# A four-layer graph network on one core: the ends of its first two layers, rearranged

## The chip, the cores and the metric

The kernel runs on one core of one Trainium2 chip, in a single launch. The metric is device time in microseconds (us). The runs of the kernel before took 5248.02, 5226.67 and 5222.31 us, with 5226.67 as their median. Durations below come from one further execution, taken with the hardware profiler.

The engines are called as in the profile: PE multiplies matrices (PEld is its loading of weights), DVE and ACT work on vectors, POOL issues the indirect DMAs that gather rows by index, and SP issues the direct DMAs. Each engine runs its own queue of instructions in order, and waits on semaphores for the others.

## What is computed

There are 6250 nodes with 256 features each, and 100000 edges (`src`, `dst`), sorted by `dst`. Four graph layers follow one another, and every one is added to its input and normalised:

```python
x = layernorm(x + L0(x))   # h = relu(layernorm(x)*gamma + beta); agg = mean of h[src] over the edges of each dst
                           # L0 = agg @ W_l.T + b_l + h @ W_r.T
x = layernorm(x + L1(x))   # attention over the edges, 8 heads, softmax over the edges of each src:
                           # s = q[src] . k[dst]; p = exp(s - max); out[src] = sum p/denom * v[dst]; out @ Wo + bo
x = layernorm(x + L2(x))   # two GAT layers of 4 heads over the edges and self loops, grouped by dst, gelu
x = layernorm(x + L3(x))   # mean over the edges of dst, two products, residual, relu
```

Layer 0 groups its edges by `dst`, in which order the input has them. Layer 1 groups them by `src`, so the kernel has to order the edges anew before layer 1 may begin.

## The kernel before

**Blocks and pieces.** Nodes are worked in 50 blocks of 125 (`NB`, `B`). The edges that end in a block have up to 16 columns of 128 slots (`CM`); what doesn't fit goes to two further columns that ten blocks share (`SH`, `GB`). A column is fetched with one indirect DMA that gathers 128 rows (`gather`, L873). A piece is a few columns of one block: 6, 6 and 4 in layer 0 (150 pieces), four times 4 in layer 1 (200 pieces). For a piece, `one_hots` (L882, DVE) makes matrices that say which slot belongs to which node of the block, and PE multiplies them with the gathered rows, which sums the rows by node in a PSUM tile `ps`. A piece is a generator; `run_pass` (L1476) starts one per step and advances every one that is under way, twice in the last ten steps. A scheduler then turns what the generators emit into one queue per engine, by estimated times and by the tiles that come free; a tile name with one buffer is handed to its users in turn.

**Layer 0.** `piece0` gathers rows of `h_table` into one of four tiles `g`. After the last piece of a block comes `finish0`: the mean `agg`; its transposition (`turned`, L856, into PSUM tile `pt`, copied out by ACT in `kept`, L861); the transposition of the block's own `h` (L1527, into `pt`); the product with `w_l` and `w_r` (`product`, L869, 8 matmuls, into PSUM tile `po`); the sum and the layer norm (`norm`, ACT at L839); a transposition of the new `x`; the products for k, v and q (12 matmuls into `po`); and two writes through SP, to `kv_table` and to `q_table` (from tile `qp`, made by `parts_of`, L823 to L826). `pt` and `po` have one buffer each.

**The ordering by source**, `by_source`, is a generator that runs beside layer 0. Its main part goes over 800 columns of 125 edges. For each, DVE makes two one-hot tiles (`oh` L1421, `o1` L1423), ACT scales one of them (`oa` L1425, `ob` L1427, for the last 200 columns `oc` L1437 too), and PE adds their products to a PSUM tile `acc` of two banks (L1432). Each group of four columns yields a cost of 3.6. After the last column DVE decodes `acc` (L1445 to L1469) into `key_s` (the node of each slot), `idx_s` (the row to gather), and the same for the shared columns (`far_s`, `near_s`). The pace is set in `beside(t)`, called after piece t has been started: the ordering is advanced until the costs it has yielded reach a number times t + 1:

```python
            def beside(t):
                if next(work_d, None) is None and t < 2:
                    next(work_d, None)
                while given[0] < 6.9 * (t + 1):
                    with tc.issue_after(last_h.ins) if given[0] < 120 else ExitStack():
                        given[0] += next(work_s, 1e9)
```

**Layer 1.** Every ten blocks `shared1` gathers the shared columns from `kv_table` and `q_table` (tile `gs`), ahead of the first piece of these blocks. `piece1` loads the block's rows of `q_table`, gathers four columns of `kv_table` into one of seven tiles `g`, turns the one-hot matrices on PE (tile `tp`), spreads `q` to the edges with them (PE, tile `qe`, two buffers), multiplies with k (DVE `prod`, L1713), sums and exponentiates (`messages`; the product with v is DVE `msg`, L1668), and sums the messages by node on PE (`ps`). After a block's last piece `finish1` follows: division by the denominators, transposition into `pt`, product with `w_o` into `pt`, sum and norm, and `features` (L1619): a further transposition into `pt`, the product with `w_gat` into `pt`, and the write of the block's row of `hs_tables[0]`, which layer 2 gathers from. `bank()` gives all of these the one buffer of `pt`. The weights `w_o` and `w_gat` are loaded when the pools of layer 1 are opened.

Of the kernel before, what the change touches and what calls it, by code (L numbers as in the profile page):

```python
# [7 lines left out]
F32 = mybir.dt.float32  # L8
I32 = mybir.dt.int32
# [646 lines left out]
def gnn_stack_kernel(ctx: ExitStack, tc: tile.TileContext, ins, out):  # L656
# [59 lines left out]
    for r in range(NR):  # L716
# [4 lines left out]
        c0 = max(0, int(place_of(g0 * GQ * EQ, -1)) // P) if g0 else 0  # L721
        reach.append((c0, min(CM, int(place_of((g1 + 1) * GQ * EQ, 1)) // P + 1)))
    DC = max(c1 for c0, c1 in reach)
    BITS = 12
    FIELD = 1 << BITS
    assert CAP + SH * P < FIELD and NB % 2 == 0
# [6 lines left out]
    with ExitStack() as fast:  # L733
# [21 lines left out]
        idx_s = const.tile([P, NB, CM], I32, name="idx_s")  # L755
        key_s = const.tile([P, NB, CH], F32, name="key_s")

        far_d, near_d, far_s, near_s = (
            const.tile([P, NGR, SH], I32, name=f"{a}_{k}") for k in "ds" for a in ("far", "near")
        )  # L760

        flags = const.tile([P, 8], F32, name="flags")
        nc.vector.memset(flags, 0.0)
        n_first = const.tile([1, 1], F32, name="n_first")
        rdens = const.tile([P, NB, 16], F32, name="rdens")
# [98 lines left out]
        def product(ps, pairs):  # L864
            n = len(pairs) * DK
            i = 0
            for aT, w in pairs:
                for k in range(DK):
                    nc.tensor.matmul(ps, aT[:, k, :], w[:, k, :], start=(i == 0), stop=(i == n - 1))  # L869
                    i += 1  # L870
# [48 lines left out]
        def by_target(pool, psum):  # L919
# [88 lines left out]
            nc.vector.tensor_tensor(ends_sb[:, 0, : EP - 1], ends_sb[:, 0, : EP - 1], ends_sb[:, 1, 1:], op=ALU.is_gt)  # L1008
            nc.vector.tensor_reduce(flags[0:1, 1:2], ends_sb[:, 0, : EP - 1], AX.X, ALU.max)
            nc.vector.tensor_copy(n_first, p_row[:, ND : ND + 1])  # L1010

        last_h = [None]

# [230 lines left out]
        def by_source(pool, work, psum):  # L1244
# [223 lines left out]
            for o, v, n in ((idx_s, low[:, :NM], CM), (far_s, low[:, NM:], SH)):  # L1468
                nc.vector.tensor_scalar(  # L1469
                    o.rearrange("p b c -> p c b"), v.rearrange("p (c b) -> p c b", c=n), float(N - 1), 0.0,  # L1470
                    op0=ALU.min, op1=ALU.max,
                )
            yield 6.0


# [15 lines left out]
        with tc.tile_pool(name="f0", bufs=1) as pool, tc.tile_pool(name="f0w", bufs=2) as work, tc.tile_pool(  # L1491
# [13 lines left out]
                nc.sync.dma_start(out=b_kv[:, k, :], in_=broadcast_rows(ins[f"L1_gnn_b{name}"], D))  # L1505
            sums, shared = {}, [None]

            def bank():
                return psum.tile([P, 512], F32, name="pt")

            def finish0(b):
                ps = sums.pop(b)[:B]
                hp = work.tile([B, 3 * D + 2], BF16, name="hp")
                move(nc.sync, hp, block_rows(h_table, b))
                nc.vector.tensor_scalar(rdeg[:, b, :], ps[:, D:], 1.0, None, op0=ALU.max)
                nc.vector.reciprocal(rdeg[:, b, :], rdeg[:, b, :])
                agg = once.tile([B, D], F32, name="agg")
                nc.scalar.activation(agg, ps[:, :D], AF.Copy, scale=rdeg[:, b, :])
                yield
                pt = turned(bank(), agg)  # L1520
                aT = kept(once, pt, "aT")
                yield
                pt = psum.tile([P, 512], F32, name="pt")[:, : DK * B].rearrange("p (k b) -> p k b", k=DK)
                for k in range(DK):
                    for i in (2, 1, 0):
                        at = i * D + k * P
                        nc.tensor.matmul(  # L1527
                            pt[:, k, :], hp[:, at : at + P], ident_b[:B, :B], start=(i == 2), stop=(i == 0)
                        )
                hT = kept(once, pt, "hT")  # L1530
                yield
                po = psum.tile([B, 3, D], F32, name="po")
                product(po[:, 0, :], [(aT, w_l), (hT, w_r)])
                yield
                o = once.tile([B, D], F32, name="o")
                nc.vector.tensor_add(o, po[:, 0, :], b_l[:B, :])
# [46 lines left out]
            def beside(t):  # L1583
                if next(work_d, None) is None and t < 2:
                    next(work_d, None)
                while given[0] < 6.9 * (t + 1):
                    with tc.issue_after(last_h.ins) if given[0] < 120 else ExitStack():
                        given[0] += next(work_s, 1e9)

            run_pass([(lambda a=a: piece0(*a)) for a in pieces((6, 6, 4))], beside)  # L1590
            for _ in work_s:
# [31 lines left out]
        with tc.tile_pool(name="f1", bufs=1) as pool, tc.tile_pool(name="f1w", bufs=2) as work, tc.tile_pool(  # L1623
            name="f1g", bufs=7
        ) as gp, tc.tile_pool(name="f1p", bufs=1, space=bass.MemoryType.PSUM) as psum:
# [3 lines left out]
            sums, held, shared, late = {}, {}, {}, []  # L1629

            def bank():
                return psum.tile([P, 512], F32, name="pt")

            def finish1(b):
                ps = sums.pop(b).rearrange("p (h c) -> p h c", h=H1)
# [52 lines left out]

            def piece1(b, c0, n):
                if c0 == 0:  # L1690
                    if b % GB == 0:
                        late.append(shared1(b // GB))
                    held[b] = work.tile([B, 3 * D], BF16, name="q")
                    move(nc.sync, held[b], block_rows(q_table, b))
                advance(late)
                q = held[b]
                g = gp.tile([P, 4, 2 * D], F32, name="g")
                for i in range(n):
                    gather(g[:, i, :], kv_table[:, :], idx_s[:, b, c0 + i : c0 + i + 1])
                st = one_hots(work, key_s[:, b, c0 : c0 + n], n, 4, 6)  # L1700
                yield
                ts = turned_hots(work, psum, st, n, 1)
                yield
                prod = work.tile([P, 4, D], F32, name="prod")
                for i0 in range(0, n, 2):
                    m = min(2, n - i0)
                    qe = psum.tile([P, 2, D], F32, name="qe", bufs=2)
                    for i in range(m):
                        for k in range(3):
                            nc.tensor.matmul(  # L1710
                                qe[:, i, :], ts[:, i0 + i, :], q[:, k * D : (k + 1) * D], start=(k == 0), stop=(k == 2)
                            )
                    nc.vector.tensor_mul(prod[:, i0 : i0 + m, :], g[:, i0 : i0 + m, :D], qe[:, :m, :])  # L1713
                yield
                msg = work.tile([P, 4 * H1, C1 + 1], F32, name="msg", bufs=3)
                yield from messages(g, n, prod, msg)
                if c0 + n == CM:
                    st_s = one_hots(work, key_s[:, b, CM:], SH, SH, 2, name="st_s")
                yield
                if c0 == 0:  # L1720
                    sums[b] = psum.tile([B, D + H1], F32, name="ps", bufs=2)
                from_all = [(c0 + i, st[:, i, :], msg, i) for i in range(n)]
                if c0 + n == CM:
                    from_all += [(CM + h, st_s[:, h, :], shared[b // GB], h) for h in range(SH)]
                for c, hot, m, i in from_all:
                    nc.tensor.matmul(  # L1726
                        sums[b], hot, m[:, i * H1 : (i + 1) * H1, :].rearrange("p h c -> p (h c)"),
                        start=(c == 0), stop=(c == CH - 1),
                    )
                if c0 + n == CM:  # L1730
                    del held[b]
                    yield
                    yield from finish1(b)

            run_pass([(lambda a=a: piece1(*a)) for a in pieces((4, 4, 4, 4))])


        beside_2 = ExitStack()
# [390 lines left out]
```

## Time and profile before

| what | value |
|---|---|
| runs | 5248.02, 5226.67, 5222.31 us |
| profiled execution: its time / its span | 5221.3 / 5219.5 us |
| mean granted clock of PE | 0.927 |
| PE, DVE, POOL busy in the span | 80%, 70%, 72% |
| gathers of h_table (layer 0): first to last | 147.6 to 1226 us |
| gathers of kv_table and q_table (layer 1) | 1297 to 2324 us |
| gathers of hs_table (layer 2, both GAT layers) | 2400 to 4482 us |
| gathers of x_table and the end (layer 3) | 4505 to 5219 us |

In the profile's groups, a row names the line, the engine and the operation, then out and in tile with their shapes; behind the bar stand the busy time in us, the mean in ns, and the engine's idle time just before such instructions, with what ended most of it:

```profile
L873 POOL DMA_INDIRECT g<-h_table_f,idx_d x800 | 799.4, 999 | 272.5 <-issue 209.3
L873 POOL DMA_INDIRECT g<-kv_table_f,idx_s x800 | 757.8, 947 | 243.7 <-issue 189.8
L1425 ACT ACTIVATE oa<-o,blk 125x128 f16<-125x128 f16 x800 | 312.4, 391 | 39.7 <-PE acc L1432 32.3
```

A waits view names for each engine what its idle time waited for: the sum, how often, and the longest. In a timeline each row is start, duration, engine, line and operation, and in brackets the idle time before it with what ended it. "Issue" is a wait for nothing that the profile shows. "PEclk" is the clock that PE was granted, as a share of full speed.

### The profile page before, as it was taken

The page shows a single profiled execution, that of the slowest core. Times are in us where ns is not written, and L with a number is a line of the kernel's source. Part 1 is how long each engine was busy: PE and PEld are TensorE (multiplying, and loading weights), DVE is VectorE, ACT ScalarE, POOL GpSimd, SP SyncE. Part 2 cuts the span into 40 slices and gives each one's busy share as a digit, 9 for nine tenths or more (in the row PEclk, how much of TensorE's full clock was granted, in tenths as well). Part 3 has the DMA queues.
Part 4 walks back from the last instruction along what each step waited for, and adds up shares of the span by engine and source line. Part 5 has one row for each costly group of instructions (what it writes and reads, how often), then busy time and mean ns, then how long its engine had stood idle before and what let it go on. Part 6 is the DMA issues. An engine that isn't in the chain of part 4 may idle for free.

```text
span 5219.5 us, 84648 instructions
## 1 busy us (share of the span) xinstructions
PE 4183.8 (80%) x27626; PEld 3140.5 (60%) x27626; DVE 3647.1 (70%) x11267; ACT 2030.5 (39%) x5923; POOL 3764.8 (72%) x3889
## 2 busy tenths in 40 slices
PE   0466899987899899886777878877777778799996
PEld 0245667765677777764666666655555656466675
DVE  7576788865899999995666666657777777423434
ACT  4011888886222222222344444434444444211212
POOL 6677777773777777764777777767777777677776
PEclk9877999997999999997999999988999899899998
DMA  5566676763777777763544444444454444788875
GB/s 132 143 161 172 185 193 189 192 181 109 222 225 227 224 224 226 226 186 85 133 130 135 133 131 132 131 116 133 133 138 135 133 136 136 196 246 243 243 211 148
DMA packets 365013, 883.96 MB, mean 169 GB/s; under 512 B 83596, under 2 KB 181954, under 8 KB 364562
## 3 DMA queue, kind: packets, MB, share of 16 engines
q0 software_dynamic: 232032, 702.40, 49.4%
q1 hardware_dynamic: 132530, 176.06, 11.4%
q8 instruction: 220, 3.60, 0.3%
q14 instruction: 231, 1.89, 0.1%
HBM read 791.50 MB, written 86.63 MB: 168 GB/s over the span
## 4 chain that ended last, share of the span: by engine, by line
POOL 28%; PE 23%; issue 19%; DVE 16%; DMA 13%; ACT 2%; SPq 0%; DVEq 0%; POOLq 0%; ACTq 0%
POOL g L873 26%; DMA g<-hs_table_f,idx_d 5%; PE ps L902 4%; PE po L869 4%; PE d L2049 3%; PE pt L869 3%; DMA g<-kv_table_f,idx_s 3%; PE acc L1432 2%; DVE st L882 2%; DMA g<-h_table_f,idx_d 2%; DVE msg L1668 2%; PE ps L1726 2%; DVE prod L1713 2%; DMA g<-x_table_f,idx_d 2%; DVE msg L1851 1%
## 5 line engine op out<-in xcount | busy, mean ns | idle before, releaser
L873 POOL DMA_INDIRECT g<-hs_table_f,idx_d x1600 | 1528.2, 955 | 487.4 <-issue 423.5
L873 POOL DMA_INDIRECT g<-h_table_f,idx_d x800 | 799.4, 999 | 272.5 <-issue 209.3
L1917 PE MATMUL ps<-msg,st 128*125 128x260 f32 x3200 | 886.9, 421 | 82.3 <-DVE msg L1851 45.4
L873 POOL DMA_INDIRECT g<-kv_table_f,idx_s x800 | 757.8, 947 | 243.7 <-issue 189.8
L902 PE MATMUL ps<-g,st 128*128 128x256 bf16 (+1 forms) x4032 | 643.8, 285 | 225.7 <-DMA g<-h_table_f,idx_d 92.6
L1917 PEld LDWEIGHTS ps<-msg,st 128*125 128x125 f32 x3200 | 642.0, 206 | 233.7 <-issue 49.9
L873 POOL DMA_INDIRECT g<-x_table_f,idx_d x544 | 515.8, 948 | 188.6 <-issue 151.7
L894 ACT CAST ts<-tp 125x512 bf16<-125x512 f32 x600 | 347.6, 580 | 752.4 <-PE tp L892 734.9
L902 PEld LDWEIGHTS <-st 128*128 128x128 bf16 x4536 | 448.9, 102 | 315.4 <-issue 182.8
L1851 DVE TENSOR_TENSOR msg<-g,pp 128x1024 f32<-128x1024 f32 x400 | 485.1, 1213 | 22.9 <-ACT pp L1848 22.7
L1845 DVE TENSOR_TENSOR e<-g,pe 128x16 f32<-128x16 f32 x400 | 68.2, 170 | 601.0 <-DMA g<-hs_table_f,idx_d 417.8
L1726 PE MATMUL ps<-msg,st 128*125 128x264 f32 x1600 | 404.1, 394 | 51.8 <-DVE ln_t L816 8.8
L882 DVE TENSOR_TENSOR st<-iota_p,key_d 128x500 f32<-128x500 f32 (+1 forms) x550 | 409.8, 745 | 41.0 <-PE ps L902 26.2
L1884 PEld LDWEIGHTS <-ts 125*128 125x128 bf16 x4800 | 179.1, 97 | 419.8 <-issue 326.8
L892 PE MATMUL tp<-ident,st 128*125 128x128 f32 x2400 | 406.4, 292 | 23.8 <-DVE st L882 16.6
L1884 PE MATMUL pe<-ad_parts,ts 125*128 125x4 bf16 x4800 | 178.5, 165 | 307.6 <-DVE e L1845 241.0
L892 PEld LDWEIGHTS tp<-ident,st 128*125 128x125 f32 x2400 | 343.7, 197 | 56.2 <-issue 23.5
L1726 PEld LDWEIGHTS ps<-msg,st 128*125 128x125 f32 x1600 | 286.8, 189 | 114.1 <-issue 45.1
L1710 PE MATMUL qe<-q,ts 125*128 125x256 bf16 x2400 | 313.4, 274 | 41.9 <-DVE prod L1713 31.0
L1788 PE MATMUL a_acc<-a_hot,a_st 128*128 128x500 f16 x950 | 300.8, 404 | 43.9 <-ACT a_row L1775 27.9
L1425 ACT ACTIVATE oa<-o,blk 125x128 f16<-125x128 f16 x800 | 312.4, 391 | 39.7 <-PE acc L1432 32.3
L1766 DVE TENSOR_SCALAR a_hot<-a_nodes,a_ends 128x500 f16<-128x500 f16 x950 | 321.8, 365 | 2.0 <-PE a_acc L1788 1.9
(401 smaller groups left out, 8202.4 us busy)
## 6 DMA issues: line engine op xcount, KB each, us to landing
g<-hs_table_f,idx_d POOLq DMA_INDIRECT x1600
a_table_f<-a_row SPq DMA_DIRECT2D x50, 437.5 KB
cnt<-a_table_f SPq DMA_DIRECT2D x50, 437.5 KB
xs<-x_table_f SPq DMA_DIRECT2D x50, 336.0 KB
g<-h_table_f,idx_d POOLq DMA_INDIRECT x800
g<-kv_table_f,idx_s POOLq DMA_INDIRECT x800
hs_table_f<-hs SPq DMA_DIRECT2D x100, 115.5 KB
own<-hs_table_f SPq DMA_DIRECT2D x100, 115.5 KB
```

The lines of the kernel that those rows point to most:

```text
L869: nc.tensor.matmul(ps, aT[:, k, :], w[:, k, :], start=(i == 0), stop=(i == n - 1))
L873: nc.gpsimd.indirect_dma_start(out=g, out_offset=None, in_=table, in_offset=bass.IndirectOffsetOnAxis(ap=idx, axis=0))
L882: nc.vector.tensor_tensor(st, iota_p[:, None, :w].to_broadcast([P, n, w]), key[:, :, None].to_broadcast([P, n, w]), op=ALU.is_equal,)
L892: nc.tensor.transpose(tp[:, i, :], st[:, i, :], ident)
L894: nc.scalar.copy(ts[:, :n, :], tp[:, :n, :])
L902: nc.tensor.matmul(ps[:, :m], st[:, i, :], g[:, i, k * D : k * D + m], start=(c0 + i == 0 and k == 2), stop=(c0 + i == CH - 1 and k == 0),)
L1710: nc.tensor.matmul(qe[:, i, :], ts[:, i0 + i, :], q[:, k * D : (k + 1) * D], start=(k == 0), stop=(k == 2))
L1726: nc.tensor.matmul(sums[b], hot, m[:, i * H1 : (i + 1) * H1, :].rearrange("p h c -> p (h c)"), start=(c == 0), stop=(c == CH - 1),)
L1766: nc.vector.tensor_scalar(hots[k][:, i, :], nodes[:, r * RW : (r + 1) * RW], ends[:, s, c : c + 1], None, op0=ALU.is_equal,)
L1851: nc.vector.tensor_mul(msg[:, : n * H2, :C2].rearrange("p (n h) c -> p n h c", h=H2), g[:, :n, :D].rearrange("p n (h c) -> p n h c", h=H2) ...
L1884: nc.tensor.matmul(pe[:, i, :], ts[:, i, :], ad_parts[:, b, k, :], start=(k == 0), stop=(k == 2))
L1917: nc.tensor.matmul(sums[b][:B, : D + H2], hot, m[:, i * H2 : (i + 1) * H2, :].rearrange("p h c -> p (h c)"), start=False, stop=(c == CH - 1),)
```

## The change

The diff has four parts.

1. **Pace.** The ordering is advanced to 7.3 instead of 6.9 per piece.
2. **More banks at the end of layer 0.** When the ordering has run out, `beside` takes the two banks of `acc` as `spare`. From then on `bank()` gives in turn one of these two or `pt`, and the block's transposition of `h` and its product with `w_l` and `w_r` go through `bank()` as well. The k, v, q products keep `po`.
3. **First gathers of layer 1.** The rows of the first 32 blocks (4000 rows, `ROWS`) hold every row that the first 8 columns of blocks 0 and 1 may name; this follows from the number of edges in front, and a new flag sends inputs for which it doesn't hold to the general path. A tile `idx_1` keeps the indices of these columns, cut to 3999, and their 16 gathers name only the first 4000 rows of `kv_table`. They so depend on the writes of blocks 0 to 31 and on `idx_1`. The first two pieces of blocks 0 and 1 come first, then the rest of the two blocks alternately, and `shared1` of the first ten blocks comes with the third piece of block 0. The pool of the tiles `g` is opened ahead of the other pools of layer 1.
4. **More banks at the end of layer 1.** When the last piece has been started, `ending` switches `bank()` to a rotation over `qe`, `tp`, `qe` and `pt`.

```diff
+    EARLY, EARLY_C = 2, 8
+    FIRST_G = min(g for g in range(1, NG + 1) if g == NG or int(place_of(g * GQ * EQ, -1)) // P >= EARLY_C)
+    FIRST_E = FIRST_G * GQ * EQ
+    FIRST_B = min(NB, -(-int(FIRST_E + 5.5 * (FIRST_E * (1 - FIRST_E / E)) ** 0.5) * NB // E))
+    ROWS = FIRST_B * B
...
+            nc.vector.tensor_scalar(
+                flags[0:1, 8:9], p_row[:, FIRST_B : FIRST_B + 1], float(FIRST_E), None, op0=ALU.is_lt
+            )
...
+            nc.vector.tensor_scalar(idx_1, idx_s[:, :2, :EARLY_C], float(ROWS - 1), None, op0=ALU.min)
             yield 6.0
...
+            spare, turn = [], [0]
+
             def bank():
-                return psum.tile([P, 512], F32, name="pt")
+                turn[0] += 1
+                k = turn[0] % 3
+                return spare[0][:, k, :] if spare and k < 2 else psum.tile([P, 512], F32, name="pt")
...
-                pt = psum.tile([P, 512], F32, name="pt")[:, : DK * B].rearrange("p (k b) -> p k b", k=DK)
+                pt = bank()[:, : DK * B].rearrange("p (k b) -> p k b", k=DK)
...
-                po = psum.tile([B, 3, D], F32, name="po")
-                product(po[:, 0, :], [(aT, w_l), (hT, w_r)])
+                po = bank()[:B, :D] if spare else psum.tile([B, 3, D], F32, name="po")[:, 0, :]
+                product(po, [(aT, w_l), (hT, w_r)])
...
-                while given[0] < 6.9 * (t + 1):
+                while given[0] < 7.3 * (t + 1):
                     with tc.issue_after(last_h.ins) if given[0] < 120 else ExitStack():
                         given[0] += next(work_s, 1e9)
+                if given[0] > 1e8 and not spare:
+                    spare.append(psum.tile([P, 2, 512], F32, name="acc"))
...
             def bank():
-                return psum.tile([P, 512], F32, name="pt")
+
+                if turn[0] is None:
+                    return psum.tile([P, 512], F32, name="pt")
+                turn[0] += 1
+                name = ("pt", "qe", "tp", "qe")[turn[0] % 4]
+                return psum.tile([P, 512], F32, name=name, bufs=2 if name == "qe" else 1)
...
                 if c0 == 0:
-                    if b % GB == 0:
-                        late.append(shared1(b // GB))
                     held[b] = work.tile([B, 3 * D], BF16, name="q")
                     move(nc.sync, held[b], block_rows(q_table, b))
+                if (b % GB, c0) == (0, made[2 * EARLY][1] if b == 0 else 0):
+                    late.append(shared1(b // GB))
...
                 for i in range(n):
-                    gather(g[:, i, :], kv_table[:, :], idx_s[:, b, c0 + i : c0 + i + 1])
+                    if b < 2 and c0 + i < EARLY_C:
+                        gather(g[:, i, :], kv_table[:ROWS, :], idx_1[:, b, c0 + i : c0 + i + 1])
+                    else:
+                        gather(g[:, i, :], kv_table[:, :], idx_s[:, b, c0 + i : c0 + i + 1])
...
-            run_pass([(lambda a=a: piece1(*a)) for a in pieces((4, 4, 4, 4))])
+
+            each = len(made) // NB
+            lead = [made[each * b + k] for b in range(2) for k in range(EARLY)]
+            lead += [made[each * b + k] for k in range(EARLY, each) for b in range(2)]
+
+            def ending(t):
+                if t == len(made) - 1:
+                    turn[0] = 0
+
+            run_pass([(lambda a=a: piece1(*a)) for a in lead + made[2 * each :]], ending)
```

More of the change, by code (lines that the diff above doesn't have):

```diff
@@ L756, in gnn_stack_kernel @@
         key_s = const.tile([P, NB, CH], F32, name="key_s")
+        idx_1 = const.tile([P, 2, EARLY_C], I32, name="idx_1")
         far_d, near_d, far_s, near_s = (
@@ L760, in gnn_stack_kernel @@
         )
-        flags = const.tile([P, 8], F32, name="flags")
+        flags = const.tile([P, 9], F32, name="flags")
         nc.vector.memset(flags, 0.0)
@@ L1531, in finish0 @@
                 yield
-                po = psum.tile([B, 3, D], F32, name="po")
-                product(po[:, 0, :], [(aT, w_l), (hT, w_r)])
+                po = bank()[:B, :D] if spare else psum.tile([B, 3, D], F32, name="po")[:, 0, :]
+                product(po, [(aT, w_l), (hT, w_r)])
                 yield
                 o = once.tile([B, D], F32, name="o")
-                nc.vector.tensor_add(o, po[:, 0, :], b_l[:B, :])
+                nc.vector.tensor_add(o, po, b_l[:B, :])
                 nc.vector.tensor_add(x_sb[:, b, :], x_sb[:, b, :], o)
@@ L1621, in features @@
             move(nc.sync, block_rows(table, b), hs)
-        with tc.tile_pool(name="f1", bufs=1) as pool, tc.tile_pool(name="f1w", bufs=2) as work, tc.tile_pool(
-            name="f1g", bufs=7
-        ) as gp, tc.tile_pool(name="f1p", bufs=1, space=bass.MemoryType.PSUM) as psum:
+        with tc.tile_pool(name="f1g", bufs=7) as gp, tc.tile_pool(name="f1", bufs=1) as pool, tc.tile_pool(
+            name="f1w", bufs=2
+        ) as work, tc.tile_pool(name="f1p", bufs=1, space=bass.MemoryType.PSUM) as psum:
             w_o = load_weight(pool, ins["L1_gnn_Wo"], "w_o")
@@ L1628, in gnn_stack_kernel @@
             w_gat = gat_weight(pool, work, 0)
-            sums, held, shared, late = {}, {}, {}, []
+            sums, held, shared, late, turn = {}, {}, {}, [], [None]
+            made = pieces((4, 4, 4, 4))
             def bank():
-                return psum.tile([P, 512], F32, name="pt")
+                if turn[0] is None:
[3 more added lines that the diff above has]
+                return psum.tile([P, 512], F32, name=name, bufs=2 if name == "qe" else 1)
             def finish1(b):
```

## The prediction

> **What bounds the kernel now.** I read the 40 slices first: POOL, which issues every gather, sits at 7 tenths almost everywhere and drops only around slices 10 and 18, the ends of layers 0 and 1. Then POOL's waits and its order of time around both dips.
>
> ```profile
> POOL gs L873 <- DMA q_table_f<-qp: 71.2, 1, 71.2
> POOL g L873 <- issue: 10.0, 33, 0.3
> ...
> POOL gs L873 <- DMA hs_table_f<-hs: 75.9, 1, 75.9
> ```
> ```profile
> 1223.51 1.16 POOL L873 DMA_INDIRECT g<-h_table_f,idx_d  x1 [0.30 <-issue]
> 1224.98 0.95 POOL L873 DMA_INDIRECT g<-h_table_f,idx_d  x1 [0.30 <-issue]
> 1297.08 0.94 POOL L873 DMA_INDIRECT gs<-kv_table_f,far_s  x1 [71.15 <-DMA q_table_f<-qp]
> ```
>
> A gather costs 0.95 us and 0.30 of issue, 1.25 in all; outside the two holes nothing else delays POOL, so it bounds layers 0 and 1 and the holes (71 and 76 us) are what the change can win. What fills the first one, by engine in stretches (columns: stretch, its length, then PE, weight loads, DVE, ACT, POOL busy with counts, granted clock, DMA share, GB/s):
>
> ```profile
> 1060.00:1100.00 40.00, 33.79 (x251) 25.00 (x249) 25.41 (x96) 31.14 (x105) 30.33 (x32) 0.91 0.65 176
> 1140.00:1180.00 40.00, 36.71 (x269) 25.91 (x267) 30.54 (x118) 39.32 (x134) 30.25 (x33) 0.92 0.65 175
> 1220.00:1260.00 40.00, 38.01 (x239) 24.47 (x238) 24.58 (x108) 37.89 (x128) 4.70 (x5) 0.86 0.22 65
> 1260.00:1300.00 40.00, 19.01 (x64) 12.98 (x63) 18.27 (x53) 7.47 (x21) 2.31 (x3) 0.63 0.20 56
> ```
>
> POOL has run out of layer 0 at 1226, ACT is full until 1262 with the ordering's last columns, then three blocks finish one by one until q_table lands at 1296. The second hole, on PE, is one period of 12.3 us that repeats:
>
> ```profile
> 2368.74 0.68 PE L856 MATMUL pt<-ident,x_sb 125*128 125x125 f32 x2 [5.36 <-ACT x_sb L839]
> 2369.87 2.12 PE L869 MATMUL pt<-w_gat,aT 128*125 128x264 f32 x4 [0.46 <-ACT aT L861]
> 2372.47 0.68 PE L856 MATMUL pt<-ident,a 125*128 125x125 f32 x2 [0.47 <-ACT hs L1619]
> 2373.60 2.07 PE L869 MATMUL pt<-w_o,aT 128*125 128x256 f32 x4 [0.46 <-ACT aT L861]
> 2381.03 0.68 PE L856 MATMUL pt<-ident,x_sb 125*128 125x125 f32 x2 [5.36 <-ACT x_sb L839]
> ```
>
> Transposes and products of several blocks share the one bank pt: from 2346 to 2397 five blocks pass through it in line.
>
> **Part 1, the pace 7.3.** No work is added; columns move forward. In PE's built order the trace's kernel has 559 ordering columns ahead of piece 116 (of 150, from 0), the changed one 608; the last of the 800 stands after piece 149 before, inside piece 143 now. When is it reached? The trace has issued 544 columns at 980 and 591 at 1020 us, so piece 116 is at about 993. From there 192 columns remain, nearly all with three ACT operations (oa, ob, oc) that start 0.29 us apart, 0.87 us a column, 167 us; the blocks' own ACT work is some 3.1 us for three pieces, 29 us for 28 pieces. ACT was 95 to 98% busy here, so 196/0.97 = 202 us: 1195. The stretch before piece 116 must also take 5% more columns; ACT has room (33 of 40 us), PE little (37 to 39 of 40). I add 10: the ordering ends at 1205 instead of 1262, from 1195 (no such loss) to 1225 (PE lets nothing forward beyond the work of pieces 143 to 149). Below nothing is excluded: no operation is added to a full engine. POOL loses little: its four tiles (some 20 us) cover PE's lag.
>
> **Part 2, three banks at the end of layer 0.** At the old end two blocks still had their k, v, q products to do, and 34 us passed to the landing of q_table (1262 to 1296.1). At the new end seven pieces and six blocks are left. In line at 12.6 us a block they would take 85. With acc's two banks and pt the built order interleaves them. Following PE's queue with the durations of the rows: pieces 143 and 144, products of the sixth-last block and the indices by +9; last gathers of h issued by +24 (below); products of the next blocks at +19, +23 and +34, sums of the last piece at +39, the last two blocks' products at +45 and +56, writes landed at +62.5. That is with 2.64 us for 12 product matmuls (at 1215 us in the chain that ended last, granted clock 1.00 from 1200 to 1220); the rows at 1273 and 1285 have 4.5 to 4.9 us. Here a rule of the Trainium skill bears on the sum, TensorE: Matmul & The Clock Gate, section What's actually happening: half clock is the default and a busy stretch of about 3.4 us lifts it. The slice at 1260 has 0.63. By the rule's warm state +62.5, at the trace's cold rows for all six blocks +75; PE has work nearly without a gap until the last block, so I take +66. q_table lands at 1205 + 66 = 1271, 25 us earlier.
>
> **Part 3, early gathers.** Sixteen gathers of blocks 0 and 1 wait for kv rows long written and for idx_1 alone. In POOL's built order the first stands ahead of the last ten gathers of layer 0 (after piece 147's), so piece 148's queue behind it until idx_1, at +8 to +13 by DVE's queue (7 us of decoding as at 1262 to 1269, and a kv addition). Piece 148's tile comes free at +9 anyway, so this costs 0 to 4; I take 1. The ten, the sixteen and three more are done before q_table lands: 19 x 1.25 = 24 us of POOL's layer 1 is out of the way. Extra operations (one comparison, one minimum) are rows of 0.15 us on DVE: nothing. Weights w_o and w_gat, formerly loaded at 1262, now queue on SP with the last block's writes; 0.4 us, within the 66.
>
> POOL is thus 25 + 24 = 49 us ahead. Seven tiles hold 28 gathers, 9 more than 19; with four shared ones they are issued 16 us after q_table, while the first tile is freed 21 after it (first message at 1317 before): 5 lost, 44 left. DVE must follow:
>
> ```profile
> DVE prod L1713 <- DMA g<-kv_table_f,idx_s: 28.5, 37, 2.1
> DVE ad_r L824 <- ACT ad_parts L823: 9.0, 20, 1.0
> DVE o L1652 <- PE pt L869: 5.8, 15, 0.8
> ```
>
> It is busy about 95% in layer 1, starts 25 us earlier (9.5 after q_table, as before), and of its waits only the first, 28.5 us, goes when POOL leads: 25 to 53. I take 40 for the gain when layer 1's messages end.
>
> **Part 4, rotating banks at the end of layer 1.** The rule of the Trainium skill, Perfetto Trace Analysis, section Matmuls, is that independent groups should rotate through PSUM banks, so that emptying one overlaps the next; no row of this trace shows several banks in this drain. By it the drain would be the last block's own path: DVE's last message at 2344, 3 us of sums, one period, landed near 2364 instead of 2399: 35 us. The built order speaks against it. The switch comes only when the last piece has begun, and by then the blocks in line have taken pt; only the last six allocations rotate. Worse, one takes qe ahead of the last piece's own qe product, so on PE and DVE, which run in order, the last piece now stands behind the pt line of blocks 45 to 48. Its cost: that line starts some 4 us earlier (the last piece's products, sum and message no longer lie in it), block 48's transposition comes at about 2378 instead of 2381; then the last piece takes qe 1.5 to 2.7, prod 1.4, sum 1.2, message 1.5, sums 3.5, normalisation 1, and the last block a period of 12.3 and a landing of 2: about 2404 against 2399. I take a loss of 5; bounds -10 to +35.
>
> **Sum.** 40 - 5 = 35 off the profiled execution, 5221.3 (span 5219.5): 5186. It lies 5.4 below the median of the three runs, 1.0 below the fastest; I add 4: 5190. Layers 2 and 3 keep their work.
>
> **Rivals.** (a) As summed, 5190, own range 5175 to 5205. (b) The lead is lost in layer 1 or the finishing doesn't overlap: DVE recovers none of its DMA waits (25 - 5 = 20), or q_table lands at +85 (16): about 5208. For it: DVE's 95%, PE's 37 of 40 before 1020. Against: 28.5 us of waits for gathers are there to recover. (c) The drain of layer 1 shortens as the rule says: 40 + 35, 5150; for it only the 12.3 us period, against it the built order. (d) Slower: the first early gather sits in POOL's queue with ten gathers of layer 0 behind it, so an ordering that ends late pushes the end of layer 0. With the sum above the gain is 1240 less the ordering's end; from 1240 on it is a loss, and if columns move in the queue but not in time (1262 as before) it is 22 us slower, 5248. For it: from 1100 on PE is busy 90% and ACT 95% or more. Against: ACT has 7 idle us of 40 before 1020, and pieces 143 to 149 no longer stand ahead.
>
> Chances: (a) 0.52, (b) 0.26, (c) 0.10, (d) 0.12. The range 5162 to 5224 leaves out most of (c) and (d). About 0.5%, 26 us, is what a measurement of this kernel tells from no change: faster by more 0.66 (a, c, some of b), within 0.25, slower by more 0.09.
>
> **What would show it.** Ordering's last column on ACT near 1205; q_table's last landing near 1271 and 19 gathers of kv done by then; POOL's hole of 71 us split into pieces of 1 to 8; no hole of PE's clock at 1260. In layer 1 DVE's waits for gathers under 15 us. At its end the last qe product after block 48's transposition, and POOL's hole before layer 2 still 75 us or more. An ordering that ends after 1240, or a second hole under 60, would make the sum wrong.

## The result, and the profile after

The changed kernel took 5181.72 us (median of four runs, 5178.58 to 5192.17) against 5224.49 for the kernel before (four runs, 5222.24 to 5248.02): ratio 0.991, interval 0.9882 to 0.9937. On a second chip, in the run z1_whole below, it took 5188.84 against 5223.98: 0.9926, interval 0.9909 to 0.9942. So 35 to 43 us are gained; 36.7 were forecast. The profiled execution is the slowest of the four, 5192.17 us, span 5190.3. Line numbers are 9 to 38 higher in the changed kernel. Three more chips, on which nine of the twelve experiments fell, run the kernel before in 6945 to 7037 us; ratios are always against the kernel before on the same chip.

POOL's waits of the changed kernel, the rows that answer to the two holes of 71 and 76 us:

```profile
POOL gs L882 <- DVE st L891: 79.3, 1, 79.3
...
POOL g L882 <- DMA kv_table_f<-kv: 12.4, 2, 12.1
```

The first hole has shrunk to 12.1 us. The second is 3.4 us longer than before; the profile there names DVE's one-hot tile of layer 2 as the releaser, where it named the write of `hs_table` before. In POOL's order of time around the first (start, duration, in brackets the wait):

```profile
1234.84 0.95 POOL L882 DMA_INDIRECT g<-kv_table_f,idx  x1 [0.30 <-issue]
...
1249.91 0.94 POOL L882 DMA_INDIRECT g<-kv_table_f,idx  x1 [0.30 <-issue]
...
1266.14 0.95 POOL L882 DMA_INDIRECT g<-kv_table_f,idx  x1 [0.30 <-issue]
1279.20 0.94 POOL L882 DMA_INDIRECT g<-kv_table_f,idx_s  x1 [12.11 <-DMA kv_table_f<-kv]
```

The first early gather stands at 1234.84, among the last gathers of layer 0, as the built order has it, and with no wait before it. The sixteenth is issued at 1266.14; the next one needs all of kv_table and waits until 1279.20.

What the faster pace costs POOL in layer 0 stands in another pair of rows, first of the kernel before, then of the changed one:

```profile
POOL g L873 <- PE acc L1432: 25.3, 56, 5.3
```
```profile
POOL g L882 <- PE acc L1445: 48.6, 56, 11.4
```

POOL waits 23 us longer for tiles that PE has still to read, and the last gather of layer 0 ends 23.7 us later than before. The stretches (PE, weight loads, DVE, ACT, POOL busy, granted clock, DMA share, GB/s) show POOL at work where it had 4.70 and 2.31 us of 40 before, and ACT free from 1220 on:

```profile
1180.00:1220.00 40.00, 36.76 (x278) 27.70 (x277) 28.58 (x110) 36.39 (x121) 22.37 (x25) 0.91 0.51 141
1220.00:1260.00 40.00, 36.72 (x229) 29.09 (x228) 24.98 (x85) 12.27 (x33) 30.57 (x32) 0.98 0.78 230
1260.00:1300.00 40.00, 21.29 (x80) 15.34 (x79) 17.18 (x37) 7.12 (x15) 21.49 (x23) 0.64 0.67 199
```

The marks of the profiled executions on chips where the kernel before takes about 5224 us, from the ACT and POOL timelines, in us from the span's start:

| mark | before | changed | z1_whole | w1_no_early | w3_one_bank |
|---|---|---|---|---|---|
| ordering's last column done on ACT | 1261.1 | 1216.7 | 1212.9 | 1217.4 | 1214.2 |
| last gather of layer 0 ends | 1225.9 | 1249.6 | 1246.9 | 1247.9 | 1245.7 |
| POOL released by the last writes | 1297.1 | 1279.2 | 1275.3 | 1280.2 | 1303.7 |
| early gathers ahead of that | 0 | 16 | 16 | 0 | 16 |
| last gather of kv ends | 2323.8 | 2286.7 | 2283.7 | 2307.3 | 2312.1 |
| first gather of layer 2 | 2399.8 | 2366.0 | 2365.3 | 2390.6 | 2390.9 |

### The profile page after: what moved, and what is told of

It is laid out like the page before. It is cut to its first block, busy times and chain, and to the rows that moved or that the text cites. A ratio compares the mean times of both kernels' runs of the same rounds, so it can differ in the third digit from the quotient of the medians.

```text
span 5190.3 us, 84722 instructions
## 1 busy us (share of the span) xinstructions
PE 4167.6 (80%) x27626; PEld 3130.5 (60%) x27626; DVE 3645.6 (70%) x11269; ACT 2029.7 (39%) x5923; POOL 3762.6 (72%) x3889
## 5 line engine op out<-in xcount | busy, mean ns | idle before, releaser
L1955 PE MATMUL ps<-msg,st 128*125 128x260 f32 x3200 | 875.6, 417 | 83.4 <-DVE msg L1889 45.6
L882 POOL DMA_INDIRECT g<-kv_table_f,idx_s x784 | 744.0, 949 | 250.6 <-issue 184.6
L1889 DVE TENSOR_TENSOR msg<-g,pp 128x1024 f32<-128x1024 f32 x400 | 485.3, 1213 | 19.7 <-ACT pp L1886 18.3
```

The source lines that it names most:

```text
L882: nc.gpsimd.indirect_dma_start(out=g, out_offset=None, in_=table, in_offset=bass.IndirectOffsetOnAxis(ap=idx, axis=0))
L1889: nc.vector.tensor_mul(msg[:, : n * H2, :C2].rearrange("p (n h) c -> p n h c", h=H2), g[:, :n, :D].rearrange("p n (h c) -> p n h c", h=H2) ...
L1955: nc.tensor.matmul(sums[b][:B, : D + H2], hot, m[:, i * H2 : (i + 1) * H2, :].rearrange("p h c -> p (h c)"), start=False, stop=(c == CH - 1),)
```

## The experiments

**z1_whole**: the changed kernel once more, so no diff.

> The changed kernel itself, on the chip of the experiments. Theory A2 (on the chip where the kernel before takes 6945 to 6951 us, PE's results reach the other engines only when POOL pauses, so POOL's lead is paid for by the others): as with the parts alone, within 0.3% of the kernel before, PE stands still for about 20 us while the early gathers are issued, and POOL's wait before layer 2 is 97 to 101 us. Rival F (the parts were each near nothing there, but together they keep their 43 us): 6900 to 6910. On a chip where the kernel before takes about 5224 us, both expect 5179 to 5192.

Measured on a chip where the kernel before takes 5223.98: 5188.84, ratio 0.9926 (0.9909 to 0.9942), as both theories said for such a chip. Which of them holds on a slower chip it doesn't tell: the whole change was not run on one.

**w1_no_early**, part 3 undone:

```diff
-                    if b < 2 and c0 + i < EARLY_C:
+                    if False:
...
-                if (b % GB, c0) == (0, made[2 * EARLY][1] if b == 0 else 0):
+                if (b % GB, c0) == (0, 0):
...
-            run_pass([(lambda a=a: piece1(*a)) for a in lead + made[2 * each :]], ending)
+            run_pass([(lambda a=a: piece1(*a)) for a in made], ending)
```

> The changed kernel without part 3, for a chip on which the kernel before takes about 5224 us and the changed one 5182 to 5189. Theory A: no gather of kv lies under the wait for q_table any more; POOL's wait before its first gather of kv goes from about 12 to 30 us and more, its last gather of kv ends 20 to 24 us later (2304 to 2311), and the time is 5203 to 5212. Rival B (DVE binds layer 1): under 8 us lost, at most 5196. Theory A3, from the slower chip (while POOL issues the early gathers, PE's results come late to the other engines, and q_table lands later by nearly as much as POOL gains): q_table lands 15 us or more earlier than in the changed kernel, and the time is within 8 us of it.

5211.12 against 5227.12: ratio 0.997 (0.9959 to 0.9981) where z1_whole, on another chip, has 0.9926: 0.44% or 23 us of the gain are gone (13 to 33 by the two intervals), and in the traces layer 2 begins 24.6 us later. POOL's wait grows from 12.1 to

```profile
1280.20 0.94 POOL L882 DMA_INDIRECT g<-kv_table_f,idx_s  x1 [32.31 <-DMA q_table_f<-qp]
```

The release is a microsecond later than the changed kernel's, and the last gather of kv is 20.6 us later, which is 16 gathers of 1.25 us to within 0.6. DVE's waits for kv rows tell where the lead goes, first here, then in the changed kernel:

```profile
DVE prod L1742 <- DMA g<-kv_table_f,idx_s: 23.4, 32, 2.2
```
```profile
DVE prod L1742 <- DMA g<-kv_table_f,idx_s: 4.6, 6, 1.2
```

Theory A holds, and B and A3 fall on this chip: POOL's lead of 20 us is taken out of 19 us of DVE's waits, and the release is not delayed in return.

**w3_one_bank**, part 2 undone:

```diff
-                if given[0] > 1e8 and not spare:
+                if False:
                     spare.append(psum.tile([P, 2, 512], F32, name="acc"))
```

> The changed kernel without part 2 (blocks of layer 0 through pt alone), for a chip on which the kernel before takes about 5224 us and the changed one 5182 to 5189. Theory A: the ordering ends near 1215 as in the changed kernel, but the blocks that are left pass in line, so that the last write of kv_table lands about 85 us after the ordering's end instead of 62, near 1298 to 1302; POOL waits 30 us or more behind the early gathers, and 17 to 23 us are lost: 5202 to 5212. Rival D (PE's work and the last gathers set the landing): it moves by under 6 us, at most 5194. Where the kernel before takes 6940 us or more: the same landing, 97 to 100 us after the ordering's end in the runs with spare banks, comes 10 to 20 us later, and the time is 0.2 to 0.4% above that of the kernel before.

5216.62 against 5225.47: ratio 0.9982 (0.9973 to 0.999), which is 0.56% or 29 us short of z1_whole's 0.9926 (20 to 39 by the two intervals), where 17 to 23 were expected. In the traces layer 2 begins 24.9 us later. From PE's order of time of this kernel:

```profile
1265.98 0.68 PE L865 MATMUL pt<-ident,x_sb 125*128 125x125 f32 x2 [3.91 <-ACT x_sb L848]
...
1279.71 0.68 PE L865 MATMUL pt<-ident,x_sb 125*128 125x125 f32 x2 [3.98 <-ACT x_sb L848]
```

Blocks follow each other at 13.7 us, not at the 12.6 of the estimate, and the release comes 89.5 us after the ordering's end, against 62.5 with three banks. It then lies 6.6 us behind that of the kernel before, though the ordering ends 47 us earlier: without the banks all of that goes into a longer line of blocks. Theory A holds, D falls. In layer 0 the rule of the Trainium skill (Perfetto Trace Analysis, section Matmuls, on rotating independent groups through PSUM banks) is thus worth some 25 us by the traces and 29 by the times; it could not be read off the trace of before.

**x1, x2, x3 and y1, y2, w2: the same parts, and the rotation, on slower chips.** x1_no_early and y1_no_early have the edit of w1, x3_one_bank that of w3. x2, y2 and w2 (no_ending) undo part 4:

```diff
                 if t == len(made) - 1:
-                    turn[0] = 0
+                    pass
```

> The changed kernel without part 3: pieces of layer 1 in their plain order, all gathers through idx_s, shared1 ahead of piece 0; pace, spare banks and the rotation at the end stay. Theory A (the lead of POOL is worth its own length): the 16 gathers and the three behind them, 19 x 1.25 = 24 us, can no longer lie under the wait for q_table; q_table lands near 1281 as in the changed kernel, POOL's first gather of kv stands there, its last one 20 to 24 us later than in the changed kernel (near 2309 instead of 2287), and the time is 5202 to 5206. Rival B (layer 1 is bound by DVE, 95% busy, so where POOL starts decides little): under 8 us lost, 5182 to 5190, and DVE's waits for gathers of kv stay below 10 us.

> The changed kernel without part 4: bank() of layer 1 stays on pt to the end. Theory A (the rotation comes too late, and its use of qe puts the last piece behind the line of blocks): the last piece's qe product goes back ahead of the transposition of block 45's x; POOL's wait before its first gather of layer 2 falls from 79.3 to about 76, and the time falls by 3 to 5 us, to 5177 to 5179. Rival C (the six rotated allocations shorten the end by letting the last two blocks overlap): the wait grows to 85 or more and the time rises by 6 to 12, to 5188 or more.

> The changed kernel without part 2: the blocks of layer 0 go through pt alone, and po is used as before; pace, early gathers and the rotation of layer 1 stay. Theory A: the ordering ends near 1217 as in the changed kernel, but the six or seven blocks that are left then pass in line at 12.6 us each, so that q_table lands at 1217 + 85 = 1302 instead of 1281; POOL stops after the 19 early gathers, and the loss is 17 to 21 us: 5199 to 5203. Rival D (PE's work and the gathers of h, which end at 1249, set the landing, not the bank): the landing moves by less than 6 us, 5182 to 5188.

> Again the changed kernel without part 3 (plain order of pieces, all gathers through idx_s); the first time it ran on a chip where the kernel before takes 6951 us. Theory A: 24 us of gathers no longer lie under the wait for q_table; POOL's last gather of kv comes 20 to 24 us later than in the changed kernel (near 2309 instead of 2287), and the time is 5202 to 5206. Rival B (layer 1 is bound by DVE, so POOL's start decides little): under 8 us lost, 5182 to 5190, with DVE's waits for gathers of kv still under 10 us.

> Again the changed kernel without part 4 (bank() of layer 1 stays on pt). Theory A: the last piece's qe product goes back ahead of the line of blocks; POOL's wait before its first gather of layer 2 falls from 79.3 to about 76, and the time falls by 3 to 5 us, to 5177 to 5179. Rival C (the rotation shortens the end): the wait grows to 85 or more, 5188 or more.

> The changed kernel without part 4, for a chip on which the kernel before takes about 5224 us and the changed one 5182 to 5189. Theory A: the last piece's qe product comes back ahead of the line of blocks, POOL's wait before its first gather of layer 2 falls from 79.3 and 81.6 to about 76, and the time falls by 3 to 6 us, 5178 to 5184. Rival C (the rotation shortens the end): the wait grows to 85 or more, and the time is 5190 or more.

| kernel | this | before, same chip | ratio (interval) | POOL's wait before layer 2 |
|---|---|---|---|---|
| x1_no_early | 6951.63 | 6951.28 | 1.0005 (0.9994 to 1.0015) | 97.1 |
| x2_no_ending | 6952.11 | 6951.28 | 0.9997 (0.9983 to 1.0011) | 98.4 |
| x3_one_bank | 6975.24 | 6951.28 | 1.0026 (1.0014 to 1.0039) | 100.3 |
| y1_no_early | 6943.03 | 6944.72 | 0.9998 (0.9987 to 1.0009) | 97.0 |
| y2_no_ending | 6952.65 | 6944.72 | 1.0003 (0.9985 to 1.0021) | 96.9 |
| w2_no_ending | 7056.99 | 7036.86 | 1.0033 (1.0021 to 1.0045) | 97.1 |

None of the expected times could be met, since they were written for the other chips. On these, with any one part gone, the kernel is within 0.3% of the kernel before. What the whole change does there was not measured, and no trace of the kernel before was taken there. The traces show two things that take the worth out of POOL's lead.

The first is in layer 1. These rows are of the changed kernel and of x1:

```profile
POOL g L882 <- DVE msg L1694: 1.5, 5, 0.3
```
```profile
POOL g L882 <- DVE msg L1694: 172.7, 42, 9.7
```

In all nine traces from these chips POOL waits 150 us or more of layer 1 for DVE to free its tiles, so it does not bound this layer, and an earlier start of its gathers need not bring an earlier end.

The second is at the end of layer 0, in x2 (PE, ACT and POOL in order of time; the early gathers are the rows of `idx`):

```profile
1679.15 0.38 PE L865 MATMUL pt<-ident,x_sb 125*128 125x125 f32 x2
1703.17 1.22 PE L878 MATMUL pt<-w_l,aT 128*125 128x256 f32 x2 [23.09 <-ACT xT L870]
```
```profile
1702.01 0.37 ACT L870 COPY hT<-acc 128x250 f32<-128x250 f32 x1 [23.83 <-remote]
```
```profile
1681.19 0.95 POOL L882 DMA_INDIRECT g<-kv_table_f,idx  x1 [0.30 <-issue]
...
1697.44 0.95 POOL L882 DMA_INDIRECT g<-kv_table_f,idx  x1 [0.30 <-issue]
```

ACT copies what PE transposed at or before 1679 only at 1702, after POOL's run of gathers has ended at 1698.4 ("remote" names no engine or queue that the profile knows of this core). ACT stands still in the same way for 23.9 us in w2 and 24.4 in y4, and for 11.9 and 7.8 us in y2; x1 and y1, without early gathers, have no such wait there. From the ordering's end to the release it takes 99.3 and 97.4 us in x2 and y2, against 78.0 and 75.7 in x1 and y1, on the same two chips. So the 20 us of gathers won are given back by a release that follows the ordering some 21 us later. No rival as written had this; A3 was formed from it, and fell on the faster chip (w1).

For part 4 these runs show no difference in POOL's wait (96.9 to 98.4 without the rotation, 97.0 to 100.3 with it). What they show of DVE's last message stands below, with part 4. A run without the rotation on a faster chip is missing.

**x4_pace69, y3_pace69**, part 1 undone, and with it most of part 2:

```diff
-                while given[0] < 7.3 * (t + 1):
+                while given[0] < 6.9 * (t + 1):
```

> The changed kernel with the pace 6.9 of before. At that pace the ordering isn't through when the last piece of layer 0 is started, so the spare banks aren't used either: what is left of the change are the early gathers and the rotation at the end of layer 1. All gathers of h stand ahead of the first early one here. Theory A: the ordering ends at about 1262 and q_table lands at about 1296 as in the kernel before; the indices are there at about 1275, so 16 to 17 gathers (20 us) lie ahead of the landing; less 3 for the rotation, 15 to 20 us faster than the kernel before, 5205 to 5210. Rival B (POOL's start decides little in layer 1): within 6 us of the kernel before, 5218 to 5225.

> Again the changed kernel with the pace 6.9, at which the spare banks aren't reached: early gathers and the rotation alone. Theory A: the ordering ends near 1262 and q_table lands near 1296 as before the change; 16 to 17 gathers lie between the indices (1275) and that landing, 20 us, less 3 for the rotation: 5205 to 5210. Rival B: within 6 us of the kernel before, 5218 to 5225.

6946.33 against 6951.28 (ratio 0.999, 0.9974 to 1.0005) and 6939.4 against 6944.72 (0.9996, 0.9979 to 1.0013): on slower chips too, so undecided for the others. The spare banks are reached after all: in both traces PE writes the last blocks' transpositions and products into `acc` once the ordering has run out, in x4 from 1713.96 on.

Here the early gathers hold nothing up. In x4 POOL issues all 16 without a break from 1720.09 to 1739.89, and in their midst DVE takes up the product of k, v and q that PE has just ended:

```profile
1726.06 1.03 PE L878 MATMUL po<-w_q,xT 128*125 128x256 f32 x4
```
```profile
1727.12 0.69 DVE L1566 TENSOR_TENSOR kv<-po,b_kv 125x512 f32<-125x512 f32 x1 [6.06 <-issue]
```

In these two runs the release follows 34.8 and 34.1 us after the ordering's end, against 36.0 in the kernel before on a faster chip. So 16 gathers lie ahead of the release at no cost that shows, and still only 5 us are won, inside the noise: a lead of POOL's is worth little on these chips even where nothing is paid for it.

**y4_two_banks_l1**, another part 4:

```diff
-                name = ("pt", "qe", "tp", "qe")[turn[0] % 4]
+                name = ("pt", "tp")[turn[0] % 2]
...
-                if t == len(made) - 1:
+                if t == 12:
                     turn[0] = 0
```

> The changed kernel with another part 4: from the 13th piece of layer 1 on, bank() alternates between tp (which gets the transpositions) and pt (which gets the products); qe isn't touched. In the built order blocks then follow one block behind the messages instead of four, and no line of blocks is left at the end. Theory A (the hole before layer 2 is a line of four blocks on one bank, formed long before the last piece): after the last sums only one transposition, block 49's own 12.3 us and a landing follow, so that POOL's wait falls from 79 to about 40 and the time is 5182 - 39 = 5143. Rival E (tp has one buffer and is needed by each piece: two more users a block hold up the pieces by 0.5 us each, 50 us over the layer): POOL's last gather of kv comes 20 to 50 us later and nothing is left of the gain, 5165 to 5195.

7230.14 against 6944.72: ratio 1.0408 (1.0385 to 1.0431). The wait before layer 2 fell by nearly as much as theory A had it, from 96.9 (y2, same chip) to 60.4. But the gathers of layer 1 ran 326 us longer (1701 us from the first shared one to the last of kv, against 1375 in y2). The two rows of PE's waits in layer 1, first of y4, then of y2:

```profile
PE tp L865 <- ACT x_sb L848: 399.1, 41, 10.9
```
```profile
PE pt L865 <- ACT x_sb L848: 52.8, 13, 7.0
```

Rival E is right that the layer pays, but it is not the buffer's occupation of 0.5 us: the transposition of x now stands in PE's queue directly behind its block's sums and ahead of the next piece, so PE waits out the layer norms. It waits 346 us more there, about the 326 by which the gathers of the layer ran longer. The lag of four blocks, which makes the line at the end, hides most of the norms before. Whether it would pay on the faster chips was not tried.

## Why the prediction was right

**Part 1, ordering's end 1205:** 1216.7 and 1212.9, within 1195 to 1225. From 1000 to 1216 ACT issued 196 columns, 1.10 us each, where the sum had 1.05 (202 us for 192): the term that was too small is ACT's share, 92% from 1020 to 1217 (181.8 of 197 us) instead of 97%. The prediction took the 95 to 98% of the stretches from 1100 on for all of it, though its own row at 1060 shows 31.14 of 40; in the changed kernel the gap lies from 1020 to 1060, with 31.96 of 40.

"POOL loses little" was wrong: its four tiles did not cover PE's lag, and the last gather of layer 0 is issued 32 us after the ordering's end instead of 24. That it did no harm is partly luck: the last piece's sums ended 38 us after the ordering, where 39 were forecast from PE's queue, 5 us behind that gather.

**Part 2, +66 to the landing:** POOL is released after 62.5 us in both traces, so the landing lies at the warm end of the two bounds. The k, v, q products show how far the clock carries. The third-last, second-last and last block in PE's order of time:

```profile
1247.18 1.13 PE L878 MATMUL po<-w_k,xT 128*125 128x256 f32 x4
1248.14 1.03 PE L878 MATMUL po<-w_v,xT 128*125 128x256 f32 x4
1249.01 1.03 PE L878 MATMUL po<-w_q,xT 128*125 128x256 f32 x4
...
1257.56 1.23 PE L878 MATMUL po<-w_k,xT 128*125 128x256 f32 x4 [0.46 <-ACT xT L870]
1258.59 1.91 PE L878 MATMUL po<-w_v,xT 128*125 128x256 f32 x4
1260.29 1.81 PE L878 MATMUL po<-w_q,xT 128*125 128x256 f32 x4
...
1269.95 2.07 PE L878 MATMUL po<-w_k,xT 128*125 128x256 f32 x4 [0.51 <-ACT xT L870]
1271.82 1.91 PE L878 MATMUL po<-w_v,xT 128*125 128x256 f32 x4
1273.53 1.91 PE L878 MATMUL po<-w_q,xT 128*125 128x256 f32 x4
```

Of these only the products of the last two blocks run at the slow rate. The last block's own products with `w_l` and `w_r`, between them in PE's queue at 1262.89, ran at 1.13 and 1.03. That there are two rates, about 1.03 and 1.91 us for four matmuls, agrees with the rule of the Trainium skill on the clock gate (TensorE: Matmul & The Clock Gate, What's actually happening); that the slow one sets in again at 1258.59, after pauses of PE of at most 1.26 us since 1246.5, came from the trace alone. The forecast that the clock's hole at 1260 goes was wrong in its place: 0.64 there after, 0.63 before; it is 1220 to 1260 that rose, from 0.86 to 0.98. The release came at 1279 and 1275 instead of 1271: the ordering ended 11.7 and 7.9 us later than summed, and the blocks behind it took 3.5 less.

**Part 3, 19 gathers, 24 us:** 16, so 20 us. The step that failed is that three further gathers would be done before q_table lands: they need the last block's rows of kv_table, whose write goes out just ahead of that of q_table. POOL was then 17.9 + 20.0 = 37.9 us ahead where 49 were reckoned; the 5 us for want of tiles did not come, and 37.1 were kept at the last gather of kv, near the 40 that were taken. DVE follows as argued, but with less room than 25 to 53: its first product of layer 1 starts at 1295.2 instead of 1308.8, 13.6 us earlier, and its waits for kv rows fall from 28.5 to 4.6, 23.9. The sum of 37.5 is about what was kept. Of these waits only 4.6 us are left to a longer lead. In w1 it is 13.2 + 5.1 = 18.3, with 16.5 kept.

The start gains 13.6 us where the release gains 17.9; the term "0.4 us" for the weights is the likely place. SP now issues them among and behind the last block's writes, and the load of the first rows of `q_table` goes out at 1281.87, 2.7 us after POOL's release, where before it followed within 0.2.

The 40 us taken for the end of layer 1's messages can be read directly, from DVE's last two messages of the kernel before, of the changed kernel and of x2, which is without the rotation:

```profile
2338.77 1.22 DVE L1668 TENSOR_TENSOR msg<-g,pp 128x1024 f32<-128x1024 f32 x1
2343.21 1.22 DVE L1668 TENSOR_TENSOR msg<-g,pp 128x1024 f32<-128x1024 f32 x1
```
```profile
2298.60 1.22 DVE L1694 TENSOR_TENSOR msg<-g,pp 128x1024 f32<-128x1024 f32 x1
2343.71 1.22 DVE L1694 TENSOR_TENSOR msg<-g,pp 128x1024 f32<-128x1024 f32 x1
```
```profile
3170.84 1.22 DVE L1694 TENSOR_TENSOR msg<-g,pp 128x1024 f32<-128x1024 f32 x1
3175.29 1.22 DVE L1694 TENSOR_TENSOR msg<-g,pp 128x1024 f32<-128x1024 f32 x1
```

The last message but one comes 40.2 us earlier. The last one does not come earlier at all, which is part 4. Rival (b), a lead lost in layer 1, falls.

**Part 4, a loss of 5:** POOL's second hole is 79.3 us in the changed kernel, 81.6 in z1, 83.3 in w1 and 78.8 in w3, all with the rotation, against 75.9 before: 3 to 7 us. PE's order of time in the changed kernel shows the step:

```profile
2337.93 0.68 PE L865 MATMUL qe<-ident,x_sb 125*128 125x125 f32 x2 [5.36 <-ACT x_sb L848]
2338.41 2.77 PE L1739 MATMUL qe<-q,ts 125*128 125x256 bf16 x12
2340.97 1.97 PE L878 MATMUL tp<-w_gat,aT 128*125 128x264 f32 x4
2345.07 3.85 PE L1755 MATMUL ps<-msg,st 128*125 128x264 f32 x8 [2.14 <-DVE msg L1694]
```

The last piece's qe product stands behind block 48's transposition, and its messages' sums follow only then. That the rotation puts it there is shown by runs: in x2, y2 and w2, without it, the last message follows the one before after 4.4 us, in the changed kernel and x1 after 45 and 44. What this costs is small, since the line of blocks takes the time in any case. From the last message but one to the start of layer 2 it takes 61.0 us in the kernel before and 65.4 to 67.5 in the four traces with the rotation; on the slower chips 63.4 or 63.5 without it and 64.0 to 66.7 with it. So the step is as forecast and the loss about the 5 us taken, though on the faster chips no run has the rotation alone removed. Rival (c), a drain shortened by the rotation, falls.

**Sum:** layer 2 began 33.7 and 34.5 us earlier, 35 were forecast. That the sum is closer than its terms is in part luck: POOL's lead was 11 us shorter than reckoned, but the 5 us for want of tiles did not come, and 40 had been taken where 44 were left. Layers 2 and 3 took 4.5 us longer in the profiled execution without a changed instruction; the runs differ by 13.6 us among themselves, so this is left open. The measured gain of 42.8 us on the prediction's chip is 6 more than forecast, and the 35.1 of z1 is 2 less. Rival (d) stayed away, since the ordering ended well ahead of 1240.

**How the gain divides:** with early gathers gone 16 us are left (5227.12 to 5211.12), with the banks gone 9 (5225.47 to 5216.62). The two losses, 23 and 29, add up to more than the gain of 35 to 43: without the banks the release even falls 6.6 us behind that of the kernel before, since the earlier end of the ordering turns into a line. The rest of the excess lies within the intervals. Parts 1 and 4 alone were not undone on a faster chip.

## What to carry to other kernels

At the end of a stage ask three things of each hole in the queue that bounds the kernel: what ends last, what then stands in line, and which work needs none of it. Moving the last producer earlier pays only if the work behind it can overlap, and work moved into the hole is worth its own length only while the engine that does it bounds the next stage and the next engine has waits of that length to give up. A rotation of buffers must begin before the line forms and must not take a buffer that the in-order engine's next urgent instruction needs, and a lag between blocks may be what hides a latency.

## What was not expected of the hardware

On three of the six chips of the experiments the same program takes 1.33 to 1.35 times as long, 6945 to 7037 us against 5224 to 5227, with a mean granted clock of 0.82 against 0.93. PE is busy 4615 us instead of 4168 (x1 and the changed kernel) and DVE 3661 instead of 3646; the rest of the 1740 us more is waiting. The longest of DVE's and ACT's waits there bear the releaser "remote", which no row of the waits on the faster chips has. In x2, w2 and y4 ACT and DVE take up PE's results only as POOL's run of gathers ends, after waits of 20 to 24 us; in x4 and y3 a run of 16 gathers holds up nothing. So POOL's gathers alone are not the cause, and what it is, and why on these chips and not the others, stays open.
